# Blocks of a top-1 expert layer in a written order over six matrix buffers, with the next layer's first eight tiles summed beside the last six blocks

## The chip, the cores and the metric

The program runs on one core of a Trainium2 chip. The metric is the time of one execution in microseconds (us), measured on the device. Engines are named as in the profile: PE (TensorE, matrix products), DVE (VectorE), ACT (ScalarE), POOL (GpSimd, which also issues indirect transfers: gathers and scatters by row numbers), SP (which issues plain transfers).

## The reference

Four layers follow each other on x, 2708 nodes of 256 features. Each has a graph part and a feed-forward part with experts. The change lies in the feed-forward part of layer 1 and the start of layer 2 (layers are counted from 0):

```
# layer 1, feed-forward: one expert of eight for each row
h    = gelu(x @ W1 + b1)                    # 2708 x 1024
p    = softmax(h @ Wg + bg)                 # 2708 x 8
e    = argmax(p)                            # the expert of the row
x    = x + p[e] * (h @ Wd[e] + bd[e])       # Wd[e]: 1024 x 256

# layer 2, graph part: attention over the neighbours
z    = norm(x) @ W                          # 256 x 256
a    = softmax over neighbours of leaky(z . attn_src + z . attn_dst)
x    = x + elu(a @ z)
```

The rows that an expert gets are known on the chip only. With this reference's inputs the eight experts of layer 1 get 354, 280, 358, 195, 359, 499, 236 and 427 rows.

## The kernel before

**Tiles.** x stays on the chip as 22 tiles of 128 rows, the last with 20. Everything is float32.

**Layer 1, hidden rows.** `send1` works three groups of tiles (0 to 7, 8 to 15, 16 to 21). For each it computes the hidden rows h, writes them to memory (`hid`), computes the gate, and `route`s: every row gets a place in a list sorted by expert, and `scatter` writes its name (row number and probability) to that place of `taken1`. `keep` is what writes the hidden rows.

**Layer 1, blocks.** A block is up to 128 rows of one expert. The class `Units` works them one after another:

- `fetch_names` gathers 128 names from `taken1` (POOL, line 527), `fetch_rows` gathers the hidden rows by them (`hs`, 512 KB, POOL, line 667). Four `hs` buffers are in turn.
- `weights1` loads the expert's matrix `wb` (1152 KB, SP, line 1077) into one of three buffers. The load is conditional: if the buffer holds that expert already it is skipped.
- `turn` transposes the hidden rows by eight PE transposes (line 678), and ACT copies them out of PSUM (line 679).
- 16 matmuls on PE (line 729) give the block's output, DVE adds the bias and multiplies by the probability (lines 730 and 731), and a `scatter` (line 513) writes the rows to `given1` in memory.

`more` decides the order in which POOL and SP issue these transfers: names while fewer than five blocks are under way, then rows while a buffer is free, then weights for two blocks ahead. `pieces` yields between the PE parts, so that `send1` of the last group can put its own products between them.

There are 9 full blocks (NA) made of the rows of the first two groups, while the third group is still being computed. They are followed by 15 blocks (ALWAYS) for what is left, taken in the order of `in_thirds`: block k of three thirds in turn, so that each third keeps to one of the three matrix buffers. Should more than 15 blocks be needed, `run_rest` works the others inside an If (line 634) whose condition was computed on the chip. Each engine that takes part in the If has its own branch instruction. On the path that is taken when the body is skipped, POOL waits for its indirect transfers and then adds to their semaphores (INC_SWDGE_SEM in the trace). After the If, everything that reads `given1` may start.

Beside the blocks, `beside(b)` hooks other work onto block b: at block NA + 4 the number of blocks still left is read and layer 2's weights are prepared, at NA + 9 it is fixed from where layer 3's small weights may be loaded.

**Layer 2, start.** Tiles are taken in six groups, FOURS: 0-1, 2-5, 6-9, 10-13, 14-17, 18-21. `turned_up` loads a group's rows of `given1` into `mine` (line 56, two buffers of four tiles), adds them to x (line 1441, by DVE for tiles 0 to 5, by POOL for the others), transposes x (line 1446), copies (line 1448) and takes the row statistics (`stats`). `valued` multiplies by W (line 267) and scales the result into `hh` (line 1464). `row_scores` and `row_factor` send the row scores through memory to have them across all partitions. `turned_up` runs one to two groups ahead of `valued`. After the last group the attention products follow (line 1548).

**What sets the order.** Within an engine, instructions run in the order in which they were written, but for `in_order`, `engine_after` and `after`, which put given instructions in another place. Waits across engines follow from which tile an instruction reads or writes; `behind` makes one load wait for given scatters.

Of the kernel before, what the change touches and what calls it, by code (L numbers as in the profile page):

```python
# [15 lines left out]
P = 128  # L16
# [3 lines left out]
E = 8  # L20
# [46 lines left out]
def adj_ffn4(ctx: ExitStack, tc: tile.TileContext, a: dict, out: bass.AP):  # L67
# [317 lines left out]
    def route(pool, hot, G, first_row, last_rows, known):  # L385
# [33 lines left out]
        ix = pool.tile([P, G, len(hot)], I32, name="r_ix")  # L419
# [3 lines left out]
    def blocks(pool, brief, known, NB, B, name, done=None, full=False, least=0):  # L423
# [26 lines left out]
        if done is not None:  # L450
            rest = pool.tile([P, E], F32, name="b_rest")
            v.scalar_tensor_tensor(rest, done, -float(B), cnt, op0=ALU.mult, op1=ALU.add)
            if least:
# [9 lines left out]
        bi = count[:, :NB, None]  # L463
        v.tensor_tensor(hot, bi.to_broadcast([P, NB, E]),
                        end[:, None, :].to_broadcast([P, NB, E]), ALU.is_ge)
# [3 lines left out]
        v.tensor_scalar(ei, eb[:, :, 0], float(E - 1), None, op0=ALU.min)  # L469
        v.tensor_tensor(vec[:, 0, :], nb[:, :, 0], end, ALU.subtract)  # L470
# [35 lines left out]
        return ei, ix, end[:, E - 1 :], nb[:, :, 0]  # L506
# [131 lines left out]
    class Units(Blocks):  # L638
# [3 lines left out]
        def __init__(self, pool, given, weights, hidden):  # L642
            Blocks.__init__(self, pool, given, weights)
            self.hidden, self.named, self.places, self.got = hidden, [], [0, 0], None

            self.names = pool.tile([P, MOST, 2], F32, name="names")
            g.memset(self.names, 1.0)
            self.hs = [pool.tile([P, HC * P], F32, name="hs", tag="hs", bufs=3) for _ in range(3)]
            for h in self.hs:
                g.memset(h, 0.0)  # L650
            self.ik, self.ok, self.outputs = "taken1", "given1", 0
# [11 lines left out]
        def fetch_rows(self):  # L663
            m, n = self.named.pop(0)
            h = self.hs[self.places[1] % len(self.hs)]
            self.places[1] += 1
            i = g.indirect_dma_start(out=h, out_offset=None, in_=self.hidden[:n, :],
                                 in_offset=bass.IndirectOffsetOnAxis(ap=m[:, 0:1].bitcast(I32), axis=0),
                                 bounds_check=n - 1, oob_is_err=False)
            self.got = i.ins.name  # L670
            self.rows.append((m, h))

        def turn(self, pool, h):
            hT = pool.tile([P, HC, P], F32, name="hTs", bufs=2)
# [7 lines left out]
        def begin(self, items):  # L682

            self.names_todo = list(items)
            self.todo = list(items)
            self.rows_todo = len(items)
            self.more(False)

        def more(self, weights=True):
            while self.names_todo and len(self.named) + len(self.rows) < len(self.hs) + 1:  # L690
                self.fetch_names(self.names_todo.pop(0))
            while self.rows_todo and len(self.rows) < len(self.hs):
                self.fetch_rows()
                self.rows_todo -= 1
            while weights and self.todo and len(self.ahead) < 2:
                self.fetch(self.todo.pop(0))

        def add(self, items):
            self.names_todo += items
            self.todo += items  # L700
# [8 lines left out]
        def pieces(self, pool, during=None):  # L709
# [4 lines left out]
            while self.rows:  # L714
                if len(self.rows) > 1:
                    turned.append(self.turn(pool, self.rows[1][1]))
                    yield
                w2, hT = self.ahead.pop(0), turned.pop(0)
                m, _ = self.rows.pop(0)
                self.more()  # L720
                if during is not None:
# [3 lines left out]
                y = (pool.tile([P, D], F32, name="ys", bufs=2) if self.outputs % 5 < 2 else  # L725
                     work.tile([P, D], F32, name="xn"))
                q = pools["psum"].tile([P, W], F32, name="yacc", bufs=2)[:, :D]
                for f in range(HC):
                    te.matmul(q, lhsT=hT[:, f, :], rhs=w2[:, f, :], start=(f == 0), stop=(f == HC - 1))  # L729
                v.tensor_tensor(y, q, w2[:, HC, :], ALU.add)  # L730
                i = v.tensor_scalar(y, y, m[:, 1:2], None, op0=ALU.mult)
                self.last = i.ins.name
                scatter(self.given, m[:, 0:1].bitcast(I32), y, self.given.shape[0] - 1, self.ok)
# [323 lines left out]
    ALWAYS = 15  # L1057
    with ExitStack() as l1:
# [5 lines left out]
        wbs, reads = {"held": []}, []  # L1064
# [5 lines left out]
        def weights1(b, e):  # L1070

            held = wbs["held"]
            if len(held) < 3:
                held.append([wbs["pool"].tile([P, 2048 + D], F32, name="wb", bufs=3), None])
            wb, was = held[b % 3]
            held[b % 3][1] = e
# [45 lines left out]
        def send1(tiles, ready=None, fill=None):  # L1122
# [3 lines left out]
            names = gt.tile([P, GM, 2], F32, name="names", bufs=1)[:, :G]  # L1126
# [84 lines left out]
            if ready is not None:  # L1211
                for _ in range(3):
                    next(fill)
            ix = route(gt, (sel,), G, t0 * P, rows(tiles[-1]), known)
            if ready is not None:
                in_order(start, (mybir.EngineType.PE,))
                keep(*was, nc.sync)
            for i, t in enumerate(tiles):
                r = rows(t)
                scatter(taken[1], ix[:r, i, :], names[:r, i, :], N - 1, "taken1")  # L1220

# [8 lines left out]
        def beside(b):  # L1230
            if b == NA + 9:
                work1.at_end = scattered["given1"][-1].name
            if b == NA + 4:
# [13 lines left out]
        for tiles in GROUPS1:  # L1247
# [83 lines left out]
            if end:  # L1331
# [7 lines left out]
                work1.hs.append(hc.tile([P, HC * P], F32, name="hs", bufs=1))  # L1339
                g.memset(work1.hs[-1], 0.0)  # L1340
                work1.more()
                between = work1.pieces(hc, lambda b: beside(b))
# [5 lines left out]
        rest = blocks(hw, gt, known, MOST - NA, P, "B", done=full[2])  # L1348
        too_many = count_left(hw, (rest[2], ALWAYS))
        gate.close()  # L1350
        past = list(scattered["taken1"])
        items = [(rest, b, past, taken[1], False) for b in in_thirds(ALWAYS)]
        more = [(rest, b, past, taken[1], False) for b in range(ALWAYS, MOST - NA)]
        work1.add(items)
        for _ in between:
            pass
        for one in wbs["held"]:
            one[1] = None
        work1.run_rest(hc, more, left[0])
# [26 lines left out]
    with tc.tile_pool(name="t3", reuse_waits="tile", bufs=1) as t3:  # L1386
# [34 lines left out]
        with tc.tile_pool(name="g2", reuse_waits="tile", bufs=1) as gp:  # L1421
# [5 lines left out]

            def turned_up(tiles):

                n, t0 = len(tiles), tiles[0]  # L1430
                adder = v if t0 < FOURS[2][0] else g
                o = gp.tile([P, 4, D], F32, name="mine", bufs=2)
                for i in load_tiles(nc, o, tiles, given[1], t0):
                    behind(i, scattered["given1"])
                xT = gp.tile([P, DC, W], F32, name="xT4", bufs=2)
                for k in range(0, n, 2):
                    r = rows(t0 + k + 1)
                    for q, m in (((P, 2),) if r == P else ((P, 1), (r, 1))):
                        i = k if q == P else k + 1
                        xs = x[:q, t0 + i : t0 + i + m, :]  # L1440
# [9 lines left out]
                return tiles, xT, stats(tiles, by_log=True)[1]  # L1450

            def valued(tiles, xT, rstd):
# [4 lines left out]
                g.memset(sc, 0.0)  # L1457
                ps = []
                for i, (t, k, r) in enumerate(own):
                    ps.append(times(xT, k, r, w_l2, D + 2, ps_acc()))  # L1460
                    s.activation(sc[:r, i, :], ps[-1][:, D:], AF.Copy, scale=rstd[:r, i : i + 1])
                lnexp(hh[:, t0 : t0 + n, D], sc[:, :n, 0], AF.Exp)
                for i, (p, (t, k, r)) in enumerate(zip(ps, own)):
                    v.tensor_scalar(hh[:r, t, :D], p[:, :D], rstd[:r, i : i + 1], hh[:r, t, D :],
                                    op0=ALU.mult, op1=ALU.mult)
# [6 lines left out]
            for k in range(len(FOURS)):  # L1472
                sc, t0, n = valued(*ahead.pop(0))
                while todo and len(ahead) < 2:
                    ahead.append(turned_up(todo.pop(0)))
                    if len(ahead) == 1:
                        row_scores(kept, sc[:, :n, 1], t0, n)
                if k > 0:
# [634 lines left out]
```

## Time and profile before

| | us |
|---|---|
| runs of the kernel before | 1919.33, 1914.12, 1907.95 (median 1914.12) |
| profiled execution | 1890.82 |
| span within it | 1889.1 |
| blocks of layer 1 on PE (944.9 to 1059.7) | 114.8, of which PE busy 107.56 |
| from the last block to the attention products (1059.7 to 1103.2) | 43.5, of which PE busy 28.90 |

The span is the time from the first to the last recorded instruction of the profiled execution, and the rest of that execution lies around it. The profiled execution was shorter than the three timed runs. Busy times are those of the trace; the granted clock of PE was 0.985 over the whole span. A line of the timeline begins with start and duration in us, then the engine, the line of the kernel, the operation, output and input by the program's names, and how many instructions it sums up; the bracket at its end is the idle time ahead of it, and what ended that. SPq, POOLq and PEldq are the instruction queues of the engines, in which branches and issues of transfers are recorded.

### The profile page before, as it was taken

The numbers are of one execution on the slowest core, as the hardware profiler recorded it, in microseconds if no ns is written. First come the engines' busy times: TensorE is split into PE (matmuls) and PEld (weight loads), VectorE is DVE, ScalarE is ACT, GpSimd is POOL, SyncE is SP. The second block draws the span as 40 slices with busy tenths as digits, with TensorE's granted clock in tenths as the row PEclk, the third lists the DMA queues.
The fourth block names the chain that finished last, engine by engine and source line by source line (L and its number), as shares of the span: only waits on it lengthen the run. The fifth ranks groups of instructions, "written<-read, shape, count | busy, mean of one in ns | idle before, by whom it ended". The sixth has DMA issues, their size and how long they took to land.

```text
span 1889.1 us, 25828 instructions
## 1 busy us (share of the span) xinstructions
PE 1816.3 (96%) x9453; PEld 1331.8 (70%) x9453; DVE 1072.4 (57%) x2451; ACT 655.3 (35%) x1472; POOL 393.3 (21%) x466
## 2 busy tenths in 40 slices
PE   8999999999999999999999699998899999999998
PEld 7888788888888888887788588887566633233344
DVE  8687872443343424444532365555345498888877
ACT  8777742222223203112322223223233542132232
POOL 0015354333321002303357400000000100011020
PEclk9999999999998999999999899999899999999999
DMA  8535658887763453644777440000101000012020
GB/s 272 156 100 165 227 193 295 320 313 295 277 265 125 141 152 103 173 119 121 209 235 250 159 65 9 1 1 1 45 1 35 17 1 23 23 26 37 23 37 18
DMA packets 93214, 237.52 MB, mean 126 GB/s; under 512 B 18288, under 2 KB 49048, under 8 KB 85017
## 3 DMA queue, kind: packets, MB, share of 16 engines
q1 hardware_dynamic: 71512, 189.18, 30.9%
q0 software_dynamic: 21568, 46.61, 9.0%
q8 instruction: 78, 1.28, 0.3%
q14 instruction: 56, 0.45, 0.1%
HBM read 218.39 MB, written 30.80 MB: 132 GB/s over the span
## 4 chain that ended last, share of the span: by engine, by line
PE 40%; DMA 4%; DVE 3%; issue 2%; ACT 1%; POOL 1%; POOLq 0%; SPq 0%; ACTq 0%; DVEq 0%
PE num L2014 10%; PE ps_acc L1548 9%; PE den L2022 6%; PE ps_tmp L375 4%; PE ps_acc L1757 3%; PE ps_tmp L267 2%; PE yacc L729 2%; DMA names<-taken,b_ix 1%; DMA hs<-hid,names 1%; DMA L_gnn_a_r<-in_L_gnn_a_r 1%; PE ps_acc L267 1%; DVE e L1985 1%; DMA mine<-given 1%; PE ps_acc L678 1%; PE ps_tmp L220 0%
## 5 line engine op out<-in xcount | busy, mean ns | idle before, releaser
L1985 DVE SCALAR_TENSOR_TENSOR e<-arena,G,mask 128x1024 f32<-128x1024 f32 (+1 forms) x252 | 275.0, 1149 | 34.1 <-PE den L2022 33.2
L2014 PE MATMUL num<-e,wh 128*64 128x512 f32 (+4 forms) x1056 | 214.0, 549 | 0.7 <-ACT L_gnn_W L1368 0.3
L1548 PE MATMUL ps_acc<-hh,e 128*128 128x257 f32 x882 | 199.2, 382 | 1.7 <-ACT o L1491 1.7
L1312 PE MATMUL acc<-sup,adrow 128*128 128x256 f32 x882 | 198.5, 382 | 1.5 <-DMA adrow<-in_adjT 1.5
L943 PE MATMUL acc<-msg,wt 128*128 128x256 f32 x882 | 197.6, 381 | 1.6 <-DVE wt L893 1.2
L1312 PEld LDWEIGHTS acc<-sup,adrow 128*128 128x128 f32 x882 | 165.1, 190 | 29.4 <-issue 5.5
L1548 PEld LDWEIGHTS ps_acc<-hh,e 128*128 128x128 f32 x882 | 163.8, 190 | 29.1 <-ACT o L1491 4.3
L943 PEld LDWEIGHTS acc<-msg,wt 128*128 128x128 f32 x882 | 165.1, 190 | 27.0 <-DVE wt L893 1.8
L591 PE MATMUL ps_acc<-xTs,wa 128*128 128x256 f32 (+1 forms) x768 | 169.3, 373 | 2.6 <-DVE xTs L581 2.6
L593 ACT ACTIVATE hTs<-ps_acc,wa 128x256 f32<-128x256 f32 (+1 forms) x192 | 88.7, 464 | 235.2 <-PE yacc L625 160.8
L625 PE MATMUL yacc<-wb,hTs 128*128 128x256 f32 x736 | 168.4, 380 | 0.0
L591 PEld LDWEIGHTS ps_acc<-xTs,wa 128*128 128x128 f32 x768 | 136.6, 190 | 28.6 <-DVE xTs L581 5.1
L2014 PEld LDWEIGHTS num<-e,wh 128*64 128x64 f32 (+1 forms) x1056 | 70.1, 136 | 122.7 <-issue 104.9
L625 PEld LDWEIGHTS yacc<-wb,hTs 128*128 128x128 f32 x736 | 137.2, 190 | 17.8 <-DVE ys L627 0.5
L1540 DVE SCALAR_TENSOR_TENSOR e<-Rb,G,mask 128x640 f32<-128x640 f32 (+2 forms) x110 | 85.0, 774 | 91.1 <-PE ps_acc L1548 90.4
L2022 PE MATMUL den<-e,wh 128*32 128x512 f32 (+4 forms) x1056 | 112.3, 546 | 0.0
L1277 DVE TENSOR_SCALAR mask<-adrow 128x1024 uint8<-128x1024 f32 (+1 forms) x66 | 41.7, 632 | 120.3 <-DMA adrow<-in_adjT 120.2
L221 ACT COPY xT<-ps_tmp 128x256 f32<-128x256 f32 x76 | 26.8, 366 | 198.9 <-PE ps_tmp L220 198.4
L729 PE MATMUL yacc<-wb,hTs 128*128 128x256 f32 x384 | 88.3, 384 | 0.8 <-DMA wb<-in_L_ffn_Wdp 0.8
L893 DVE SCALAR_TENSOR_TENSOR wt<-adrow,wt 128x640 f32<-128x640 f32 (+3 forms) x67 | 71.1, 1063 | 25.4 <-ACT wt L141 25.1
L2022 PEld LDWEIGHTS den<-e,wh 128*32 128x32 f32 (+1 forms) x1056 | 33.1, 109 | 73.6 <-issue 69.6
L513 POOL DMA_INDIRECT given<-ys,xs x46 | 65.8, 1431 | 81.1 <-DVE ys L628 67.9
(472 smaller groups left out, 2631.0 us busy)
## 6 DMA issues: line engine op xcount, KB each, us to landing
adhalf<-in_adjT SPq DMA_DIRECT2D x42, 677.0 KB
wb<-in_L_ffn_W2p SPq DMA_DIRECT2D x24, 1152.0 KB
wb<-in_L_ffn_Wdp SPq DMA_DIRECT2D x24, 1152.0 KB
wa<-in_L_ffn_W1b SPq DMA_DIRECT2D x24, 1028.0 KB
adrow<-in_adjT SPq DMA_DIRECT2D x42, 512.0 KB
adrow<-in_adjT SPq DMA_DIRECT2D x42, 320.0 KB
adrow<-in_adjT SPq DMA_DIRECT2D x21, 576.0 KB
adrow<-in_adjT SPq DMA_DIRECT2D x21, 448.0 KB
```

The lines of the kernel that those rows point to most:

```text
L375: te.matmul(p[:, :w], lhsT=w1[:, c, f * P : (f + 1) * P], rhs=xnT[:, c, c0 : c0 + w], start=(c == 0), stop=(c == DC - 1))
L591: i = te.matmul(p[:, f % 2, : m * P], lhsT=w1[:, c, f * P : (f + 1) * P], rhs=xT[:, c, : m * P], start=(c == 0), stop=(c == DC - 1))
L593: s.activation(hT[:, f, : m * P], p[:, f % 2, : m * P], AF.Gelu, bias=bias[:, f : f + 1])
L625: te.matmul(q[:, k, :], lhsT=hT[:, f, k * P : (k + 1) * P], rhs=w2[:, f, :], start=(f == 0), stop=(f == HC - 1))
L729: te.matmul(q, lhsT=hT[:, f, :], rhs=w2[:, f, :], start=(f == 0), stop=(f == HC - 1))
L943: te.matmul(p[:q, n - pair[0], :], lhsT=wt[:, k : k + q], rhs=msg[:r, j, :], start=(j == 0 and n == pair[0]), stop=(j == FULL - 1 and n == ...
L1312: te.matmul(p[:q, n - pair[0], :], lhsT=ad[:, k : k + q], rhs=sup[:, jj, :], start=(jj == 0 and n == pair[0]), stop=(jj == FULL - 1 and n ...
L1540: i = v.scalar_tensor_tensor(e[:r, :w], Rb[:r, c0 : c0 + w], G[:r, j, :], mask[:r, j, c0 : c0 + w], op0=ALU.max, op1=ALU.mult)
L1548: te.matmul(p[:, : D + 1], lhsT=e[:, k : k + q], rhs=hh[:, j, :], start=(j == 0), stop=False)
L1985: v.scalar_tensor_tensor(e[:, :w], slow[:, m % 2, k, :w], G[:, j, 2 * pair + k, :], mask[:, j, c0 : c0 + w], op0=ALU.max, op1=ALU.mult)
L2014: te.matmul(num[k * DK : (k + 1) * DK, hf, :q], lhsT=wh[some, j, 2 * pair + k, :DK], rhs=e[some, :q], start=(j == 0), stop=(j == FULL), ti ...
L2022: te.matmul(den[z * Q : (z + 1) * Q, :q], lhsT=wh[some, i, 2 * pair + k, DK : DK + 1] .to_broadcast([some.stop - some.start, Q]), rhs=e[so ...
```

## The change

1. **Order and number of the rest blocks.** `blocks` takes the rest's experts from the last to the first, and also tells after how many rest blocks all rows of tiles 0 to 7 are done (`last`). The rest blocks run in a written order, REST1, of pairs (block, buffer) over six matrix buffers, three of them new; an expert's blocks use one buffer. `fetch_rest` loads up to three matrices ahead, and not into a buffer that is still to be read.
2. **Names and routing.** At the beginning three names are gathered, then one ahead while full blocks run, and three ahead in the rest. The last group is routed after two more pieces of the blocks, not three, and what DVE does to write its last hidden rows (`keep`) may not come ahead of the third routing instruction. At the last full block the next turn stands inside the products, ahead of the last four matmuls.
3. **The If moves.** `run_rest` at the end is gone. Ahead of block 18 `branch` stands: an If which, if there are more than 15 rest blocks or if tiles 0 to 7 are not done after 9 of them, works the last 12 items one by one. After it SP loads tiles 0 to 3 and 4 to 7 of `given1` (512 KB each).
4. **Layer 2's first tiles.** DVE adds these eight tiles beside blocks 21 and 22, and their statistics (of tiles 0 to 5) are taken at block 23. At the start of layer 2 they are only transposed and multiplied. Tiles 8 to 13 are then added by DVE, 14 to 21 by POOL. The group 6-9 is transposed in two halves, the second (`finish`) in the middle of `valued` of the group before.

The core of the diff:

```diff
@@ blocks
+        if early is not None:
+            begins = pool.tile([P, E], F32, name="b_begin")
+            v.tensor_scalar(begins, end, -1.0, end[:, E - 1 :], op0=ALU.mult, op1=ALU.add)
...
+        v.tensor_scalar(rest, until[:, :, 0], 0.0, None, op0=ALU.is_gt)
+        v.tensor_tensor(begins, begins, until[:, :, 0], ALU.add)
+        v.tensor_tensor(begins, begins, rest, ALU.mult)
+        last = pool.tile([P, 1], F32, name="b_last")
+        v.tensor_reduce(last, begins, AX.X, ALU.max)
+        return ei, ix, end[:, E - 1 :], last
@@ Units
         def begin(self, items):
...
+            for _ in self.hs:
+                self.fetch_names(self.names_todo.pop(0))
             self.more(False)
 
         def more(self, weights=True):
-            while self.names_todo and len(self.named) + len(self.rows) < len(self.hs) + 1:
-                self.fetch_names(self.names_todo.pop(0))
             while self.rows_todo and len(self.rows) < len(self.hs):
+                if not self.named:
+                    self.fetch_names(self.names_todo.pop(0))
                 self.fetch_rows()
                 self.rows_todo -= 1
+            while self.names_todo and len(self.named) < (3 if self.places[1] >= self.border else 1):
+                self.fetch_names(self.names_todo.pop(0))
             while weights and self.todo and len(self.ahead) < 2:
                 self.fetch(self.todo.pop(0))
+            if weights and not self.todo:
+                self.fetch_rest()
+
+        def fetch_rest(self):
+            while self.rest and len(self.rest_ahead) < 3:
+                n, k = self.border + self.at[1], REST1[self.at[1]][1]
+                if max((i for i in range(n) if buffer_of(i) == k), default=-1) >= self.now:
+                    break
+                self.rest_ahead.append(self.weights(self.border + self.at[1], expert_of(self.rest.pop(0))))
+                self.at[1] += 1
...
-        def pieces(self, pool, during=None):
+        def pieces(self, pool, during=None, ahead=None):
...
             while self.rows:
-                if len(self.rows) > 1:
+                split = None
+                if ahead is not None and n in ahead:
+                    ahead[n]()
+                    split = len(nc.cur_bb.bb.instructions)
+                late = n == self.border - 1
+                if len(self.rows) > 1 and not late:
                     turned.append(self.turn(pool, self.rows[1][1]))
                     yield
-                w2, hT = self.ahead.pop(0), turned.pop(0)
+                w2, hT = (self.ahead or self.rest_ahead).pop(0), turned.pop(0)
@@ layer 1
+    REST1 = [(0, 3), (4, 4), (6, 2), (1, 3), (5, 4), (7, 2), (2, 3), (8, 2), (3, 3),
+             (9, 5), (10, 1), (11, 4), (12, 0), (14, 2), (13, 0)]
...
             if ready is not None:
-                for _ in range(3):
+                for _ in range(2):
                     next(fill)
-            ix = route(gt, (sel,), G, t0 * P, rows(tiles[-1]), known)
+            routed = len(nc.cur_bb.bb.instructions)
+            ix = route(gt, (sel,), G, t0 * P, rows(tiles[-1]), known, hw)
             if ready is not None:
                 in_order(start, (mybir.EngineType.PE,))
+                ranked = [k.name for k in nc.cur_bb.bb.instructions[routed:]
+                          if k.engine == mybir.EngineType.DVE][2]
+                kept = len(nc.cur_bb.bb.instructions)
                 keep(*was, nc.sync)
+                engine_after(kept, mybir.EngineType.DVE, ranked)
...
         def beside(b):
-            if b == NA + 9:
+            if b == NA + AHEAD1 + 1:
                 work1.at_end = scattered["given1"][-1].name
+            if b in (NA + ALWAYS - 3, NA + ALWAYS - 2):
+                first = len(nc.cur_bb.bb.instructions)
+                for t0 in EARLY[::2][(b - NA - ALWAYS + 3) * 2 :][:2]:
+                    add_early(t0)
+                engine_after(first, mybir.EngineType.DVE, work1.last)
+            if b == NA + ALWAYS - 1:
+                for some in FOURS[:2]:
+                    prepared[some[0]] = stats(some, by_log=True)[1]
...
-        items = [(rest, b, past, taken[1], False) for b in in_thirds(ALWAYS)]
-        more = [(rest, b, past, taken[1], False) for b in range(ALWAYS, MOST - NA)]
-        work1.add(items)
+        items = [(rest, b, past, taken[1], False) for b in range(MOST - NA)]
+
+        def branch():
+
+            with tc.If(left[0] > 0):
+                work1.all_again(hc, items[AHEAD1:], wbs[3][0],
+                                slice(NA + AHEAD1, NA + ALWAYS))
+            pin(scattered["given1"][-1].name)
+            wbs[3][1] = None
+            known_rows = list(scattered["given1"])
+            for t0, o in zip(EARLY[::4], work1.early):
+                for i in load_tiles(nc, o.rearrange("p (t d) -> p t d", d=D), range(t0, t0 + 4),
+                                    given[1], t0):
...
+                    behind(i, known_rows)
+
+        def add_early(t0):
+
+            o = work1.early[t0 // 4].rearrange("p (t d) -> p t d", d=D)
+            xs = x[:, t0 : t0 + 2, :]
+            v.tensor_tensor(xs, xs, o[:, t0 % 4 : t0 % 4 + 2, :], ALU.add)
+
+        work1.add([items[b] for b, _ in REST1])
         for _ in between:
             pass
-        for one in wbs["held"]:
-            one[1] = None
-        work1.run_rest(hc, more, left[0])
@@ layer 2, turned_up
-                adder = v if t0 < FOURS[2][0] else g
-                o = gp.tile([P, 4, D], F32, name="mine", bufs=2)
-                for i in load_tiles(nc, o, tiles, given[1], t0):
-                    behind(i, scattered["given1"])
+                adder = v if t0 < FOURS[4][0] else g
+                late = [t for t in tiles if t not in EARLY]
+                if late:
+                    o = gp.tile([P, 4, D], F32, name="mine", bufs=2)
+                    for i in load_tiles(nc, o, late, given[1], t0):
+                        behind(i, scattered["given1"])
```

Where the If's body is skipped, what it computes is the same as before; `all_again` gathers, loads, turns, multiplies and scatters for each of its items.

## The prediction

> **What bounds** the kernel now. I read the page first: engines, then the 40 slices.
>
> ```profile
> PE 1816.3 (96%) x9453; PEld 1331.8 (70%) x9453; DVE 1072.4 (57%) x2451; ACT 655.3 (35%) x1472; POOL 393.3 (21%) x466
> ...
> PE   8999999999999999999999699998899999999998
> ```
>
> TensorE (PE) is busy for 96% of the span, and one slice only falls to 6 tenths: the 23rd, 1039 to 1086 us. That is where layer 1's last blocks end and layer 2 begins, which is what the diff touches. So the change can only win idle PE time around there. PE's timeline of 970 to 1104 us has nearly all of it in these gaps and one of 0.52 at 1010.91:
>
> ```profile
> 984.79 1.35 PE L678 MATMUL ps_acc<-ident,hs 128*128 128x128 f32 x8 [4.19 <-DMA hs<-hid,names]
> 985.94 5.06 PE L729 MATMUL yacc<-wb,hTs 128*128 128x256 f32 x16
> ...
> 1005.87 1.07 PE L678 MATMUL ps_acc<-ident,hs 128*128 128x128 f32 x8 [1.68 <-DMA hs<-hid,names]
> ...
> 1052.66 7.14 PE L729 MATMUL yacc<-wb,hTs 128*128 128x256 f32 x32 [0.84 <-DMA wb<-in_L_ffn_Wdp]
> ...
> 1071.55 1.12 PE L1446 MATMUL ps_tmp<-ident,x 128*128 128x128 f32 x4 [11.75 <-DVE x L1441]
> ...
> 1087.15 2.88 PE L267 MATMUL ps_acc<-w_l,xT 128*128 128x258 f32 x12 [1.78 <-DVE hh L1464]
> ...
> 1103.17 0.70 PE L1548 MATMUL ps_acc<-hh,e 128*128 128x257 f32 x2
> ```
>
> The bracket is the idle time and what ended it. The last block ends at 1059.73; I call it T. Layer 2's attention products (L1548) start at 1103.17, so the **boundary** costs 43.4 us. Its PE work is 88 matmuls L267 of 0.217 us each and 44 transposes of 0.11: 19.1 + 4.8 = 24 us. About 19 us are lost, 11.75 in one gap. The chain of waits shows what fills it:
>
> ```profile
> 1051.23 15.21 DMA L_gnn_a_r<-in_L_gnn_a_r
> ...
> 1067.21 3.57 DMA mine<-given
> 1070.81 0.70 DVE x L1441
> 1071.53 3.86 DMA mine<-given
> 1075.39 0.07 issue
> 1075.46 2.51 POOL x L1441 x2
> 1077.99 4.06 DMA mine<-given
> ```
>
> The outputs of the blocks (`mine`) are loaded 512 KB at a time into two buffers, added by DVE (0.7 us per two tiles) or POOL (1.25), and one load waits for the add that frees its buffer. The first starts 7.5 us after T. The instructions of the If at L634, over the span:
>
> ```profile
> L634 POOLq EVENT_SEMAPHORE  x8: 17/43/2521, 592.6 to 1064.0; - x8
> ...
> L634 PEldq COMPARE_BRANCH  x2: 327/2100/3872, 588.7 to 1056.2; - x2
> ...
> L634 POOLq INC_SWDGE_SEM  x2: 955/1684/2413, 595.5 to 1064.1; - x2
> ```
>
> (min/median/max in ns.) Block 23's scatter, issued at 1060.93, lands at 1064.0; POOL then spends 2.41 us in the If's other path, and only at 1066.5 may SP load. PE's branch ran at 1056.2 under earlier matmuls and cost it nothing; layer 0's took 3.87 us and left a gap of 2.1.
>
> The **block stretch** runs from 944.94 to T, 114.8 us for 24 blocks. Its PE work is 24 x 3.46 (L729, 16 matmuls) + 22 x 0.87 (L678) + 1.5 routing + 0.9 centring = 104.5, so some 10 us are lost: 4.19, 1.68, 0.84, 0.52, and some 1.9 in which the instructions after the first gap run slowly.
>
> **The skill** on this. "TensorE: Matmul & The Clock Gate", Part 1: the clock falls to half after an idle window of about 3.4 us and needs as long a busy one to recover. The trace agrees: after the 4.19 us gap the turn (8 transposes) takes 1.35 as listed (else 1.04, of which 0.87 until the next starts) and the 16 matmuls 5.06 (else 3.62); the granted clock is 0.84 over the boundary, 0.99 over the blocks. "DMA: Bandwidth & Descriptors", Anatomy of one DMA: 2.0 us fixed plus bytes / 436 GB/s, so by its price 3.2 us for 512 KB; `mine` took 3.57 to 4.06, a gathered `hs` of the same size 4.6 in the median and up to 10.71 with other loads in flight. "Advanced Engine Details and Errata", Control Flow Timing: 0.108 us for a compare-and-branch. True here of SP, ACT, DVE and POOL (0.05 to 0.07), not of PE (0.33 and 3.87), so I price PE's branch by the trace.
>
> **Part 1: weights and order of the rest.** By the reference's inputs, worked out from its gating, the experts hold 354 280 358 195 359 499 236 427 rows; 9 full blocks take 2 1 2 1 2 1 0 0 of them, and the rest needs 1 2 1 1 1 3 2 4 = 15 blocks. Conditional loads of 1.15 MB really made: 15 of 24 before, 11 after, since an expert's blocks share a buffer. That removes 4 x 1.18 = 4.7 MB of some 28 in the stretch. On PE it removes the 0.84 wait and relieves the gathers. Six buffers let three loads run ahead, so no weight is late.
>
> **Part 2: names and routing.** The 4.19 gap is a series on POOL's side, in the chain of waits:
>
> ```profile
> 973.04 3.75 DMA names<-taken,b_ix
> ...
> 979.97 4.69 DMA hs<-hid,names
> ```
>
> Six scatters of names leave from 957.86 to 965.3; when they have landed, the first rest names are gathered at 973.04, their rows at 979.97, landed 984.66. The change routes one piece of the blocks sooner and holds the writing of hidden rows behind the first routing steps, so these scatters leave about one block (4.33) earlier: just over the 4.19, which goes with its slow clock (-6.1), and with fewer loads in flight so do 1.68 + 0.52. But behind the scatters POOL now issues name gathers for the two last full blocks one at a time, each followed by an `hs` gather that waits for it, then three names for the rest and another such wait. A landing is 3.75 when free, 8.65 (1002.85) when loaded; three in series are 11 to 26 us on POOL, against a lead of four `hs` buffers, about 4 x 4.33 = 17 us less the 4.6 of the gather itself. PE stall: 0 to 13, I take 3. POOL's own 3.97 us a block (three indirect DMAs, 1.02 + 0.31 each) against PE's 4.33 lets it catch up by only 0.36 a block.
>
> **Part 3: the branch moves** from the end to ahead of block 18, PE's between block 17's products and a turn. It is no longer hidden: its gap is 0.3 to 2.4 (L634's extremes), I take 1.0. Behind POOL's copy stand the `hs` gathers of blocks 22 and 23. POOL waits until block 17's scatter has landed (3.1 after issue) and then 1 to 2.4 in the other path, so block 22's rows are issued some 6.9 us after block 17 and needed after three blocks and a turn, 13.0 + 1.0. That leaves 7 us for a landing of 4.6 to 10.7 beside the two early `mine` loads (1 MB) and a weight load: stall 0 to 4, I take 0.7. SP's queue has the early `mine` ahead of three weight loads, two of them skipped; the third has three blocks of lead. The taken path (12 blocks anew) needs more than 15 rest blocks, or rows of tiles 0 to 7 beyond the ninth; the counts are 15 and 7. Layer 3's small loads (nine DMAs) stand before the scatters of blocks 19, 22 and 23 and take some 6 us of POOL, as they did before; I add 0.5.
>
> Sum of the stretch: 9.1 lost in the named gaps before, 1.0 + 3 + 0.7 + 0.5 = 5.2 after: **-4** (0 to -7.5; beyond 0 in rival B).
>
> **Part 4: the boundary.** Tiles 0 to 7 are loaded from outputs that are final by block 17 and summed by DVE beside blocks 21 and 22: four adds of 0.7 on an engine 29% busy there (33.64 of 114.8), statistics of six tiles (0.6 each) beside block 23. If that cover were gone it would be 6 us behind T. After T, PE has 16 transposes and up to 32 matmuls without waiting: 1.8 + 6.9 less what is queued behind later tiles, 6 to 8 us. No idle of 3.4 us is left, so the clock holds. The late loads need block 23's landing, not the 2.41: issue at T + 5.0, tiles 8 and 9 land (256 KB) at T + 8.6. Then DVE's adds, 0.7; POOL's are left for tiles 14 to 21, whose loads wait for a buffer until about T + 10 and T + 11.5, land 4 later, are added (2.5) by T + 19.5; then transposes, copy and four tiles' L267 (0.9 + 0.4 + 3.5), `hh` (2): L1548 at about T + 29. PE's own sum is 24 + 1.4 wait + some 4 of small gaps, the same. 43.4 - 29.2 = **-14** (-10 to -16: at best T + 27, at worst the POOL chain is 4 late). Layer 2's products, 194.76 of 197 us busy from 1103 on, are bound by PE and have no wait to swallow the shift, which reaches the end whole.
>
> **Sum:** -4 - 14 = -18 (-11 to -23). The profiled execution took 1890.82 us (span 1889.1 and 1.7 around it), 1.2% below the median of the runs, 1914.12; on its own scale 1873. On the runs' scale I take 18 x 1.012 = 18: **1896**.
>
> **Rivals.** A, the forecast, 0.62. B, the mid-stretch drain and the serial names land at the loaded 8.65 and 10.71: stall 8 to 12 instead of 3.7, and the boundary wins 10 to 12: -5 to -10 in sum, 1904 to 1909; 0.2. For it: POOL is nearly as slow as PE here. Against: 4.7 MB less in flight. C, gains cancel within half a per cent, through B with a boundary bound by POOL's adds: about 1911, 0.08. D, slower: the same queue of POOL, but with names issued behind waiting gathers so late that each of the six or so blocks behind the full ones waits a whole loaded landing: 6 x (8.65 - 4.33) = 26, less the 14: +12, 1926. It decides where stalls exceed 18 us; 0.07. E, the branch is taken: 12 blocks in series at names 4 + rows 4.6 + turn and products 4.3 + output 3 = 16 us, +175, 2090; only if my counts are wrong, 0.03, outside the range.
>
> **The numbers.** About 0.5%, 9.6 us, is what a measurement can tell from no change. A and the better half of B lie beyond: faster 0.81, same 0.10, slower 0.09. The range, 1885 to 1910, takes A's worst and best (-11 to -23, with the runs' own spread of 6 above and below) and most of B.
>
> **To look for** in the changed profile: slice 23 rises to 8 or 9; no single PE idle above 4 us after the last L729; L1548 26 to 31 us after it; the first late `mine` issued 4 to 6 us after it; data on the hardware queue 4 to 5 MB less; PE's branch with under 2.5 us; turns behind the full blocks with waits of 3 us in sum on `hs`. I am wrong if those waits exceed 10 us, if block 22 waits over 4, or if L1548 comes later than T + 34.

## The result and the profile after

The changed kernel took 1905.2 us (median of 9 runs, 1898.25 to 1911.3), the kernel before 1914.12 (9 runs, 1907.17 to 1919.33). The ratio is 0.995, with a 95% interval of 0.9929 to 0.9972: some 9 us faster, where 18 were forecast.

The first two traces can't be subtracted. The profiled execution of before took 1890.82, 23 us less than the median of its runs; that of after took its median, 1905.2. Layer 0, which the change leaves alone, was already some 14 us later in the second (its If's branch on PE began at 603.1 instead of 588.7). So I compare stretches inside the traces here, and whole times only by ratios. Most of the further runs below lie on chips where before takes 1893 to 1896.

The page of after, engines, slices, and the queue that carries the weights:

```profile
PE 1822.0 (96%) x9453; PEld 1333.3 (70%) x9453; DVE 1074.7 (56%) x2467; ACT 656.6 (34%) x1472; POOL 388.5 (20%) x460
...
PE   8999998999998999999988999999899999999998
...
q1 hardware_dynamic: 70936, 184.46, 29.8%
```

The slice of 6 tenths is gone, but two slices of 8 stand ahead of its place (the 21st and 22nd, 952 to 1047 us): the idle time has moved from behind the blocks to between them. The queue moved 184.46 MB instead of 189.18, which is four loads of 1.18 MB less. PE's timeline of after, with the idle time ahead of a line in the bracket:

```profile
984.72 1.97 PE L708 MATMUL ps_acc<-ident,hs 128*128 128x128 f32 x8 [6.95 <-ACT hTs L709]
...
1015.05 0.63 PE L708 MATMUL ps_acc<-ident,hs 128*128 128x128 f32 x4 [3.35 <-DMA hs<-hid,names]
...
1063.77 1.94 PE L708 MATMUL ps_acc<-ident,hs 128*128 128x128 f32 x8 [3.57 <-PEq L1467]
...
1083.51 7.07 PE L781 MATMUL yacc<-wb,hTs 128*128 128x256 f32 x32
...
1098.57 0.63 PE L1592 MATMUL ps_tmp<-ident,x 128*128 128x128 f32 x4 [2.42 <-DVE x L1587]
...
1118.94 0.70 PE L1723 MATMUL ps_acc<-hh,e 128*128 128x257 f32 x2
```

The last block ends at T = 1090.58, and the attention products begin 28.4 us later (43.4 before); the one marked idle time left in between is 2.42, where the longest was 11.75. The chain of waits of after shows the new end path:

```profile
1091.72 2.69 DMA given<-xn,names
...
1095.08 4.06 DMA mine<-given
1099.14 0.03 issue
1099.17 0.69 DVE x L1587
```

No drain stands between the scatter's landing (1094.4) and the load, which leaves at T + 4.1 instead of T + 7.5. But ahead of T there are new gaps, one of them PE's branch ("PEq L1467": PE's own queue stood at the If), and the slow clock after them: turns of 1.97 and 1.94 where 1.04 is usual.

### The profile page after: what moved, and what is told of

Its sections match the earlier page's. It is cut to its first block, busy times and chain, and to the rows that moved or that the text cites. A ratio compares the mean times of both kernels' runs of the same rounds, so it can differ in the third digit from the quotient of the medians.

```text
span 1903.5 us, 25846 instructions
## 1 busy us (share of the span) xinstructions
PE 1822.0 (96%) x9453; PEld 1333.3 (70%) x9453; DVE 1074.7 (56%) x2467; ACT 656.6 (34%) x1472; POOL 388.5 (20%) x460
## 3 DMA queue, kind: packets, MB, share of 16 engines
q1 hardware_dynamic: 70936, 184.46, 29.8%
## 5 line engine op out<-in xcount | busy, mean ns | idle before, releaser
L1723 PEld LDWEIGHTS ps_acc<-hh,e 128*128 128x128 f32 x882 | 163.7, 190 | 29.2 <-ACT o L1666 4.2
L649 PE MATMUL yacc<-wb,hTs 128*128 128x256 f32 x736 | 170.9, 384 | 5.6 <-DVE ys L651 2.9
L781 PE MATMUL yacc<-wb,hTs 128*128 128x256 f32 x384 | 90.9, 392 | 0.0
```

The lines of the kernel that those rows point to most:

```text
L649: te.matmul(q[:, k, :], lhsT=hT[:, f, k * P : (k + 1) * P], rhs=w2[:, f, :], start=(f == 0), stop=(f == HC - 1))
L1723: te.matmul(p[:, : D + 1], lhsT=e[:, k : k + q], rhs=hh[:, j, :], start=(j == 0), stop=False)
```

## Experiments

All ratios are to the kernel before, with 95% intervals.

**Both kernels again.** No edit; on one chip.

> The kernel before, unchanged, for a second trace. Its first profiled execution took 1890.8 us, 23 us less than the median of its runs, so the traces of before and after can't be subtracted as they stand. Theory (stalls by execution): an ordinary execution of before, 1907 to 1919 us, loses some 20 us more than the first trace, spread over layers 0 and 1 in stretches that the change doesn't touch, with PE's products late without a wait; the boundary from the last block to the attention products stays at 43 +- 2 us. Rival (the first trace is ordinary, timing adds 20 us around the span): span of this execution again about 1890 us.

> The changed kernel, unchanged, for a second trace. The first shows the boundary at 28.5 us (43.4 before) but three long losses among the blocks: 6.95 us at 977.8, some 4.4 at 1011 to 1016, 3.57 at PE's branch. Theory: the first is a stall of this execution and not of the program, so it is elsewhere or absent in a second trace; the branch's gap is the program's and comes back at 3 to 4 us; ratio to before 0.993 to 0.997. Rival: all three belong to the program and come back at the same blocks.

Before: 1892.99, ratio 1.0002 (0.9993 to 1.0011), profiled 1890.48. Changed: 1883.83, ratio 0.9949 (0.9933 to 0.9964), profiled 1887.25. My theory for before was wrong: 1890 is ordinary on this chip, and its runs lie there too. The level differs by chip, or by session, which these runs don't separate; the ratio does not. What PE waited for from 935 to 1125 us (sum, times, longest), first before, then changed:

```profile
PE ps_tmp L1446 <- DVE x L1441: 11.1, 2, 10.5
PE ps_acc L678 <- DMA hs<-hid,names: 7.2, 1, 7.2
PE ps_acc L267 <- DVE hh L1464: 1.8, 1, 1.8
```

```profile
PE ps_acc L708 <- DMA hs<-hid,names: 9.6, 2, 9.2
PE ps_acc L708 <- PEq L1467: 3.9, 1, 3.9
PE ps_tmp L1592 <- DVE x L1587: 1.8, 1, 1.8
```

| stretch, us | before | changed |
|---|---|---|
| start to the first block's products | 946.2 | 948.5 |
| first block's products to T | 115.7 | 123.4 |
| T to the attention products | 42.1 | 28.1 |
| attention products to the end | 784.7 | 785.5 |

So the boundary gains 14.0, and the blocks lose 7.7 of it; what the two traces differ by ahead of the blocks (2.3) I can't put down to the change. Of the three gaps of the first trace, the branch came back (3.9) and so did a wait for rows, with 9.2 ahead of block 7's products (blocks counted from 0): PE turns block 8's rows there, those of the last full block. Before, the 7.2 were for block 9's, the first of the rest. The 6.95 did not come back on this chip, and nothing in the first trace tells what held PE there. It is not of one execution alone, though: the run with two Ifs apart, on a chip where before takes 1907, has 4.48 us at the same turn.

```profile
982.21 1.97 PE L708 MATMUL ps_acc<-ident,hs 128*128 128x128 f32 x8 [4.48 <-ACT hTs L709]
```

(The two executions differ by 3.3 us in span, the medians by 9: the changed kernel's was the slowest of its six runs.)

**Nothing early.** The last block's boundary without tiles 0 to 7 summed ahead:

```diff
-    EARLY, prepared = GROUPS1[0], {}
+    EARLY, prepared = (), {}
```

> The changed kernel with tiles 0 to 7 loaded, added and measured after the last block like the others (nothing early; DVE adds tiles 0 to 13); branch, order of blocks and buffers as in the changed kernel. Theory (early sums carry the boundary's gain): boundary 36 to 41 us against 28.5, so 8 to 12 us slower than the changed kernel, about equal to before. Rival (the gain comes from the If's drain, 2.4 us, and from DVE instead of POOL adding tiles 6 to 13): boundary 29 to 33 us.

1893.59, ratio 1.0006 (0.9998 to 1.0014): 9.8 us slower than the changed kernel on the same chip. T to the attention products 36.6, and the wait for the first late sum:

```profile
PE ps_tmp L1592 <- DVE x L1587: 7.5, 2, 7.0
```

The theory held. Of the boundary's 14.0 us, 8.5 are the early tiles; the other 5.5 are what else the change does there, the drain that is gone and DVE in POOL's place above all, which no run takes apart. In this run's time nothing of the 5.5 is left: its blocks take 121.8 from the first products to T, 6.1 more than before.

**No If.**

```diff
-            with tc.If(left[0] > 0):
-                work1.all_again(hc, items[AHEAD1:], wbs[3][0],
-                                slice(NA + AHEAD1, NA + ALWAYS))
```

> The changed kernel without the If ahead of block 18: the path for more than 15 rest blocks is left out, with it the branches of all engines and POOL's drain. Theory (the branch is the mis-sized term: 3.57 us gap on PE and about 1.6 of slow clock after it): 4 to 6 us faster than the changed kernel, ratio to before 0.992 less than it, about 0.9925, and no idle of PE over 1 us ahead of block 18's turn. Rival (the branch falls into time that is lost anyway, because gathers of rows behind it set the pace): under 2 us.

1886.11, ratio 0.9964 (0.995 to 0.9978): not faster than the changed kernel, in the median 2.3 us slower, with intervals that overlap. PE's waits:

```profile
PE ps_acc L708 <- DMA hs<-hid,names: 8.7, 3, 4.6
PE yacc L781 <- DMA wb<-in_L_ffn_Wdp: 3.3, 2, 2.6
```

The branch's gap is gone, and waits for weights and rows stand in its place. SP's two early loads left at 1055.0, eleven us after block 17's products, the weights of block 22 stood behind them in SP's queue, and PE waited 2.6 us for these. The rival was nearer. This trace is of the slowest of its runs, so it names the new waits but does not size them.

**Names three ahead**, for the full blocks too:

```diff
-            while self.names_todo and len(self.named) < (3 if self.places[1] >= self.border else 1):
+            while self.names_todo and len(self.named) < 3:
```

> The changed kernel with names gathered three ahead for the full blocks as well (the diff's one ahead), so that the names of the last two full blocks leave before the scatters of the routing. In the changed kernel's second trace POOL stands 5.19 us for a names landing (973.87 to 979.36) ahead of the rows of block 7, and PE then waits 9.2 us. Theory (serial names): PE's wait at block 7 falls by 4 to 6 us, the kernel is 4 to 7 us faster than the changed one, ratio to before about 0.992. Rival (queued weight loads): the rows leave 5 us earlier and land no sooner, since five weight loads of 1.15 MB fill the queues from 970 to 990; less than 2 us.

1877.1, ratio 0.9906 (0.9882 to 0.993); the interval lies just outside that of the changed kernel (from 0.9933, on another chip). First block's products to T: 116.3 instead of 123.4. POOL's timeline of the changed kernel, second trace, shows what was removed:

```profile
973.87 1.05 POOL L551 DMA_INDIRECT names<-taken,b_ix  x1 [0.30 <-issue]
980.11 1.02 POOL L693 DMA_INDIRECT hs<-hid,names  x1 [5.19 <-issue]
```

POOL stood for 5.19 us (the bracket names no cause, but the names landed at 979.4, 5.5 us after they were sent for), then sent for block 8's rows, which landed 9.4 us later. With the edit these two gathers are blocks apart, and PE waits for no full block's rows. What is left is a wait for block 10's, ahead of block 9's products:

```profile
PE ps_acc L708 <- DMA hs<-hid,names: 4.2, 2, 3.9
```

The theory of serial names held, and this version is faster than before and, by its ratio, than the changed kernel.

**Weights held back, alone and with the names.**

```diff
             after(i, reads[-1])
+            if b in (NA, NA + 1):
+                behind(i, [work1.gots[NA - 1]])
```

(`gots` keeps the gathers of rows.)

> The changed kernel with the first two weight loads of the rest held back until the rows of the last full block have landed. Now five real loads stand from 969 to 990, and the rows of block 7, issued at 980.1, take 9.4 us instead of some 4.5. Theory (burst of weights): these rows land in 5 to 7 us, PE's wait at block 7 falls by 3 to 4, and the held loads are still in time for blocks 9 and 10; ratio to before 0.992 to 0.993. Rival (serial names, or the three other loads are enough to fill the queues): less than 1.5 us.

> Both: names three ahead for the full blocks, and the rest's first two weight loads held back behind the last full block's rows. If serial names and the burst each cost what their theories say, PE's wait at block 7 goes wholly (9.2 us and slow clock after it, together 9 to 12) and the ratio to before is 0.988 to 0.990. If one of them alone bounds, it is no better than the better of the two single edits.

Alone 1881.88, ratio 0.9949 (0.9928 to 0.997); with the names 1875.87, ratio 0.9913 (0.9888 to 0.9938). The burst is real: five loads between 970 and 990 in the changed kernel. The stretch as a row (length, busy time of PE, weight load, DVE, ACT and POOL, granted clock, busy share of the DMA engines, GB/s):

```profile
975.00:990.00 15.00, 5.44 (x29) 4.33 (x28) 1.56 (x4) 1.07 (x2) 4.03 (x4) 0.83 0.96 359
```

Rows gathered in it took 9.4 us, those of the other blocks between 946 and 1032 us 4.0 to 5.4. With the loads held back the wait for block 8's rows fell from 9.2 to 4.5 us, by somewhat more than the theory had it, but the ratio did not follow. In the traces, holding back shortened the first block's products to T to 118.6 alone and 113.9 with the names; the ratios show nothing of it. I leave it at: no gain that these runs can tell.

**A short body.** The If's body with one item of twelve:

```diff
-                work1.all_again(hc, items[AHEAD1:], wbs[3][0],
+                work1.all_again(hc, items[AHEAD1 : AHEAD1 + 1], wbs[3][0],
```

> The changed kernel with one item instead of twelve in the body of the If that is skipped (the path for more blocks is left out but for one). The branch, its place, POOL's drain and all waits stay; PE jumps over 48 recorded instructions instead of 576. Theory (PE's branch costs by the length of what it jumps over, since 288 took 0.33 us and 576 and more took 3.5 to 7): branch below 1 us, PE's idle ahead of block 18's turn below 0.5 instead of 3.9, and 2 to 6 us faster than the changed kernel. Rival 1 (the place decides: PE waits for its own earlier products at the branch): 3.5 to 4 us of idle as before. Rival 2 (idle goes, but weights and rows behind SP's and POOL's branches are late in its place, as without the If): same time as the changed kernel.

1881.42, ratio 0.9943 (0.9926 to 0.9961). PE's branch in the changed kernel (min/median/max in ns), and then in this one:

```profile
L1467 PEldq COMPARE_BRANCH  x1: 7012/7012/7012, 1037.6 to 1037.6; - x1
```

```profile
L1467 PEldq COMPARE_BRANCH  x1: 218/218/218, 1031.8 to 1031.8; - x1
```

The idle time at it falls from 3.9 to 0.3, and from block 17's products to block 19's it is 9.2 us instead of 14.5: the branch costs 5.3 us of PE, the clock included. The place among the blocks is the same, so it is the code jumped over that does it. Some 0.9 comes back at block 22, where PE waits for an early sum on DVE. The ratio is only 0.0006 lower, within its interval, so that the whole 5 us reach the end is not shown.

**Two Ifs of six items**, with names three ahead: one behind the other (alone, and with the weights held back), and with four blocks between them, ahead of blocks 14 and 18. The edit of the first two, beside that of the names:

```diff
+            half = AHEAD1 + 6
             with tc.If(left[0] > 0):
-                work1.all_again(hc, items[AHEAD1:], wbs[3][0],
+                work1.all_again(hc, items[AHEAD1:half], wbs[3][0], slice(0, 1))
+            with tc.If(left[0] > 0):
+                work1.all_again(hc, items[half:], wbs[3][0],
```

> The changed kernel with names three ahead for the full blocks, and the twelve items of the If divided over two Ifs of six, one behind the other at the same place, so that PE jumps twice over 288 recorded instructions; nothing is left out. Theory (branch by length): both branches of PE about 0.3 us, idle ahead of block 18 below 1 us instead of 2.9 to 3.9, and with names three ahead a ratio to before of 0.987 to 0.990. Rival (two jumps add up to the same instructions, or POOL drains twice, 2 to 5 us more for the rows of block 22): idle as before or a wait at block 22, ratio 0.990 to 0.993.

> The same, and the rest's first two weight loads held back behind the rows of the last full block. Holding back alone gave nothing that could be told from the changed kernel. Expected within 2 us of the run without it; more only if those rows now set the pace, then 2 to 3 us better.

> The changed kernel with names three ahead, and the If's twelve items divided over two Ifs of six with four blocks of work between them: one ahead of block 14, one ahead of block 18; nothing is left out. With the two Ifs one behind the other the first jump took PE 0.34 us and the second 4.29 with 4.8 us idle. Theory (a short jump is cheap when PE's instructions behind it have had time to be fetched): both branches 0.2 to 0.4 us, no idle of PE over 1 us at either, ratio to before 0.985 to 0.989. Rival 1 (the second of two jumps is dear wherever it stands, since what lies behind it was never fetched): 3.5 to 5 us idle at block 18. Rival 2 (POOL's second drain is the price): PE waits 3 to 6 us for rows at blocks 17 to 19 in its place, ratio 0.990 to 0.993.

Together 1881.79, ratio 0.9926 (0.9911 to 0.994), and with weights held back 1881.72, 0.9934 (0.9918 to 0.9951); apart 1898.83 on a chip where before takes 1907.44, 0.9945 (0.9925 to 0.9965). None is better than one If with names three ahead. PE's two branches, together:

```profile
L1468 PEldq COMPARE_BRANCH  x1: 339/339/339, 1030.6 to 1030.6; - x1
```

```profile
L1470 PEldq COMPARE_BRANCH  x1: 4287/4287/4287, 1034.2 to 1034.2; - x1
```

and apart, 3.77 and 6.02 us:

```profile
L1470 PEldq COMPARE_BRANCH  x1: 3772/3772/3772, 1032.1 to 1032.1; - x1
```

Six items took 0.34 us ahead of the second If, 4.29 in it, and 3.77 and 6.02 apart. So length alone is not the rule. The Trainium skill, "Runtime: NRT & Kernel Launch", section Instruction fetch mechanics, says that instructions are fetched ahead in blocks of 16 KiB, and that a taken branch to a place outside of the two that are there has to fetch it before it goes on. The traces agree: among the transfers of the changed kernel's second trace from 1037.6 to 1046.5, the dear branch and 1.9 us behind it, stand two such fetches, one of them within the branch,

```profile
q8 instruction: 2, 0.03, 1.6%
```

and none from 1030.5 to 1034.1 in the run with two Ifs together, its cheap branch, but again two from 1034.1 to 1039, its dear one. Over all traces, PE's 25 branches of 3.4 us and more, layer 0's among them, each have one or two such fetches within them, and the five of 0.22 to 0.34 us have none, where a whole execution has 78 in some 1890 us. For which engine a fetch is made the traces don't say. Where a jump's end lies in those blocks would then decide with its length; I did not move it by itself, so that this is not shown.

**Rest order and buffers undone**, with nothing early:

```diff
-    REST1 = [(0, 3), (4, 4), (6, 2), (1, 3), (5, 4), (7, 2), (2, 3), (8, 2), (3, 3),
-             (9, 5), (10, 1), (11, 4), (12, 0), (14, 2), (13, 0)]
+    REST1 = [(k * 5 + i, k) for i in range(5) for k in range(3)]
```

> As the run with nothing early, but the rest's blocks in the order of thirds over three matrix buffers, as before the change (experts from the last to the first). 9 of the 15 rest loads are real in that order, against 5 in the written order over six buffers. Theory (fewer loads relieve gathers and weights): PE's waits for weights and rows among blocks 9 to 23 grow by 2 to 5 us, ratio to before 1.002 to 1.004 against 1.0006 of the run with nothing early. Rival (the rest's loads lie beside other work, and the losses are at block 7 and at the branch): within 1 us of it.

1895.11, ratio 1.0003 (0.9993 to 1.0013), against 1.0006 with the written order. The queue is back at its 189.18 MB, and the total is the same: first products to T 121.3, against 121.8. That is what the rival said, but the waits of PE don't let the four loads go for nothing. With the written order (the run with nothing early), and then with thirds:

```profile
PE ps_acc L708 <- DMA hs<-hid,names: 8.9, 2, 8.6
PE ps_acc L708 <- PEq L1467: 3.8, 1, 3.8
```

```profile
PE ps_acc L708 <- DMA hs<-hid,names: 7.6, 3, 3.6
PE yacc L781 <- DMA wb<-in_L_ffn_Wdp: 1.9, 1, 1.9
PE ps_acc L708 <- PEq L1465: 1.4, 1, 1.4
```

Among blocks 9 to 23 the waits of the theory are there with thirds, 0.5 and 3.5 us for the rows of blocks 9 and 10 and 1.9 for the weights of block 23; with the written order there are none. Against them stand a shorter wait for full blocks (3.6 for block 7's rows, where 8.6 went to block 8's) and a cheaper branch: over the same twelve items it took 4.45 us instead of 6.87, and from block 17's products to block 19's it was 10.3 us instead of 14.3. So the equal totals don't price the loads; what four of them are worth stays open.

## Why the prediction was right, and where it was not

- **Part 4, the boundary: right in mechanism and size.** 14.2 forecast, 14.0 measured on one chip; the attention products at T + 29.2 forecast, T + 28.1 and T + 28.4 found; the first late load at T + 5.0 forecast, 3.8 and 4.1 found. It reaches the end: behind it 784.7 and 785.5 us. The run with nothing early shows that the early sums carry most of it. Of the two paths that were held equally long, PE's own work is the one that set the end: POOL's adds were done by T + 17, not T + 19.5, and PE did not wait for them.
- **Part 1: four loads less, as worked out, but their value is not shown.** The waits for weights among the blocks (0.8 and 0.5 in the traces of before) are gone in those of the changed kernel. How far the gathers were relieved is open too (the run with thirds); the crowd that hurts most is that of the last full blocks, which the change leaves.
- **Part 2: the term that failed.** I set -6.1 and -2.2 for gaps removed and +3 for serial names. The sign of the sum was wrong: the waits for rows went from 7.2 to 9.6 us on one chip. I had bounded this stall at 0 to 13 and taken 3; 9.2 came in one piece, for the last full block's rows behind their own names, and the run with names three ahead took 7.1 off the blocks. But that run still waits 4.2 us for rows, so the gaps would not all have gone without the serial names either.
- **Part 3: the branch was mis-sized.** Taken 1.0, bounds 0.3 to 2.4; measured 3.9 of idle and 5.3 with the clock. The upper bound was a misreading: PE's own line for L634 goes to 3.87, and 2.4 is POOL's INC_SWDGE_SEM. Nor would the two branches of one trace have bounded it: the changed kernel's took 6.65 and 7.01, since how much code is jumped over, and by the fetches probably where it lies, sets the price. Block 22's rows, for which I had added 0.7, were in time.
- **The sum.** Blocks: -4 forecast, +7.7 in the pair of traces, about +5 if the boundary's 14 and the median's 9 are taken. Part 2's miss (2.4 for -5.3) and the branch's (5.3 for 1.0) are about the 11.7 by which the traces' blocks missed. That is rival B's stall, "8 to 12 instead of 3.7", and its whole time (1904 to 1909), but with the boundary's full gain and not the 10 to 12 that it gave. That the time lay in the range is no merit of the sum: the range held it because it reached to B.
- **The signs to look for.** Slice, boundary and megabytes came as written, the late load at 4.1 in the first trace (3.8 in the second). "PE's branch with under 2.5 us" did not come, and "waits of 3 us in sum on `hs`" only in the first trace (3.3, beside the 6.95), not in the second (9.6, just under the 10 that would have been the sign of being wrong).
- **The clock and two prices.** The clock gate of the Trainium skill, "TensorE: Matmul & The Clock Gate", Part 1, is seen again: after 3.9 us idle the next 16 products took 5.31 instead of 3.62. But 3.4 us is no safe bound here: in the run with names three ahead and weights held back, 2.86 us of idle were enough, and the granted clock was 0.50 in the turn that followed.

```profile
988.36 1.94 PE L709 MATMUL ps_acc<-ident,hs 128*128 128x128 f32 x8 [2.86 <-DMA hs<-hid,names]
```

At the boundary, where I wrote that the clock holds as no idle of 3.4 us is left, it held after 2.42. The 0.108 us for a compare-and-branch, which I called true of SP, ACT, DVE and POOL, is more than these traces show for them (0.05 to 0.07). And the price of 3.2 us for 512 KB is given for transfers that POOL issues, so that it is to be held against the gathered `hs` and not against `mine`, which SP issues; neither figure stands in a sum.

## What to carry to other kernels

When loads are put ahead of others on one queue, count each wait for a landing that the queue's own order makes: on POOL, names one ahead of their rows cost some 8 us more than names three ahead (by the ratios; 7.1 in the traces). Work pulled from behind a last wait to beside earlier blocks came in as counted, since the engine that does it had time there; a conditional moved from an end into a stream of matmuls has to be priced by the code that it skips. When one edit changes two waits at once, equal totals don't show that either is free: look at the waits. And before two traces are subtracted, see whether the parts that were not changed take the same time.

## What the runs showed of the hardware that I had not expected

- A skipped If took PE between 0.22 and 7.0 us of branch. Under matmuls still running (the end of before) it cost nothing, in a stream of them 0.3 to 4.9 us of idle time; over the same twelve items it took 4.45 to 7.01 us in different kernels. The other engines' branches took 0.05 to 0.07.
- The slow clock followed marked idle times of 2.82 to 2.95 us in four places (turns of 1.94 instead of 1.04, granted clock 0.50), not after 2.42 at the boundary and 2.52 at a branch.
- The same kernel (before) has medians of 1892.8, 1893.0, 1895.7, 1907.4 and 1914.1 us in the five sessions. In two traces of the slower ones PE stands 6.95 and 4.48 us at the same turn without a wait that accounts for it; what holds it there is not shown.
- In the changed kernel's second trace an indirect gather of 512 KB took 4.0 to 5.4 us between 946 and 1032 us, but 9.4 among five weight loads and 6.0 to 9.5 later, beside other loads; one of 1 KB of names 2.5 to 4.6, and 5.5 to 8.8 in such crowds.
